# Twelve products without a reader behind layer 0's MLP, and four buffers for the key chunks of the first and the last image

## The chip, the cores and the metric

The kernel runs on one core of one Trainium2 chip. The metric is the time of one execution on the device, in microseconds (us). The time before is the median of three runs; one further execution was taken with the hardware profiler, and all stages below are read from it.

## What is computed

Four images of 192 channels and 64 x 64 pixels go through four layers, one after the other. Cut to what matters here:

```
# layer 0: deformable-convolution queries, channel attention, then an MLP per pixel
xs2 = shortcut + attention(xn)
h1  = layer_norm(xs2, gamma2, beta2)
xs3 = xs2 + gelu(h1 @ w_fc1 + b_fc1) @ w_fc2 + b_fc2        # 192 -> 768 -> 192

# layer 1: non-local attention over all 4096 pixels of an image
g_x, theta_x, phi_x = (conv1x1(x, w, b) for w, b in ...)     # 192 -> 96 each
f   = softmax(theta_x^T phi_x)                                # 4096 x 4096
x   = conv1x1(g_x f^T, W_w, W_b) + x

# layer 2: overlapping-window attention and a gated MLP;  layer 3: a masked depthwise convolution
```

Layer 1 of an image needs all of layer 0's output of that image.

## The kernel before, in words

All arithmetic is float32. The images are taken one after the other, but the layers of neighbouring images are woven together: while layer 1 of image b runs, the gathers of layer 0 for image b+1 run beside it (`weave`); while layers 2 and 3 of image b end (`rest`), the MLP of layer 0 for image b+1 (`mlp0`) is taken a step at a time between their pieces. Image 0's MLP has nothing beside it.

`mlp0` (from L688) goes over eight chunks of 512 pixels. `attend` (L715 to L731) adds the attention's output, a norm follows, `widen` (L796, L803) makes 768 hidden channels with a Gelu on ScalarE (L809), and `narrow` brings them back to 192. `narrow(1)` makes the last 64 channels (L821), `narrow(0)` the first 128 (L818: six products of 128 x 512); each ends with one VectorE instruction (L825) that reads the product's PSUM tile `p` and adds bias and residual into `x`. The PSUM tiles come from a pool of five buffers. After `narrow(0)` the chunk is written to the table `x_flat` in device memory by three DMAs on SyncE's queue (L844).

`keys` (from L849) reads that table back in eight chunks of 512 pixels: each a tile `xk` of 96 x 2 x 512 from the pool `l1k`, loaded by one DMA of 384 KB on SyncE's queue (L855). Of a chunk it makes the keys `ph` (`tp`, L858: two products of 96 x 512, copied out by ScalarE at L859) and the values `gx` (`g`, L863: eight products of 96 columns, copied out by VectorE at L866). Each float32 product shows as two PE instructions in the profile. A buffer of `l1k` is free when the last product of its chunk has read it, and only then can the load that takes its place be issued[...].

In images 1 and 2 the norms of the next image's `offsets` are made between the chunks of `keys` (L360 to L348) from loads of their own (L431). In images 0 and 3 `keys` runs alone. `layer1` follows: its input chunks `xc` (L899), the queries `th` (L902, copied at L904), the scores `s` (L910, copied out by ScalarE at L912), running maxima on VectorE (L915, L917), exponentials and the products with `gx` (L976).

The order of the instructions on each engine is made by a planner, from the order in the program, the data that each needs and its own costs; parts of layer 2's code are kept in the order written. The planner does move work ahead: products of `layer1` (`th`) stand between the chunks of `keys` in the trace. Waits and the reuse of memory are worked out from the tiles.

`ident` is a 128 x 128 identity matrix and `bias` a constant of 128 x 384 (layer 2's position bias, loaded from 174 to 213 us of the span); both stay in SBUF for the whole kernel.

Of the kernel before, what the change touches and what calls it, by code (L numbers as in the profile page):

```python
# [18 lines left out]
B, C, H, W = 4, 192, 64, 64  # L19
# [6 lines left out]
NCH = 8  # L26
# [53 lines left out]
def conv_seq_kernel(ctx: ExitStack, tc: tile.TileContext, a, out: bass.AP):  # L80
    nc = tc.nc

    def pool_of(**kw):

        return tc.tile_pool(**({} if kw.get("space") == DRAM else {"reuse_waits": "tile"}), **kw)
# [7 lines left out]
    def const(shape, name):  # L93
        return wpool.tile(shape, F32, tag=name, name=name)
# [40 lines left out]
    ident = const([128, 128], "ident")  # L135
# [382 lines left out]
    def gather(b, s, at, m2, kept=None):  # L518
# [166 lines left out]
            nc.scalar.copy(m2[rows, C + 2 * M + Q * q : C + 2 * M + Q * q + Q], pm[rows, M:C])  # L685
        yield

    def mlp0(b, m2, pool, sb, ps):  # L688


# [4 lines left out]
        def parts(sb, at, dram, to):  # L695

            yield sb[:, 0 : 2 * at], dram[0:M, to : to + 2 * at]
            for q in range(2):
                yield sb[Q * q : Q * q + Q, 2 * at :], dram[M:C, to + at * q : to + at * q + at]

        def load(i):
            x = xs[i] = pool.tile([M, 3 * HN], F32, tag="x", name=f"xa_{b}_{i}", bufs=2)
            for to, of in parts(x, HN, a["x"][b].rearrange("c h w -> c (h w)"), CN * i):
                nc.sync.dma_start(out=to, in_=of)
# [6 lines left out]
        def attend(i):  # L711

            x, xn = xs[i], xns.pop(i)
            p = ps.tile([128, CN], F32, tag="h", name=f"o_{b}_{i}_0")
            nc.tensor.matmul(  # L715
                p.rearrange("p (r c) -> p r c", c=W), lhsT=m2[:, 0:M], rhs=xn[:, 0:8, 1:65], start=True, stop=False,
                skip_group_check=True,
            )
            for q in range(2):
                nc.tensor.matmul(  # L720
                    p[:, bass.ts(q, HN)].rearrange("p (r c) -> p r c", c=W), lhsT=m2[:, C + M * q : C + M * q + M],
                    rhs=xn[:, 8:12, 1:65], start=False, stop=True, skip_group_check=True,
                )
            nc.vector.tensor_tensor(x[:, 0:CN], x[:, 0:CN], p, ALU.add)
            p = ps.tile([128, CN], F32, tag="h", name=f"o_{b}_{i}_1")[:, 0:HN]
            for q in range(2):
                nc.tensor.matmul(
                    p[Q * q : Q * q + Q].rearrange("p (r c) -> p r c", c=W), lhsT=m2[:, M:C], rhs=xn[:, 4 * q : 4 * q + 4, 1:65],
                    start=True, stop=False, skip_group_check=True,
                )  # L730
            nc.tensor.matmul(  # L731
                p.rearrange("p (r c) -> p r c", c=W), lhsT=m2[:, C + 2 * M :], rhs=xn[:, 8:12, 1:65], start=False, stop=True,
                skip_group_check=True,
            )
            nc.vector.tensor_tensor(x[:, CN:], x[:, CN:], p, ALU.add)
            if i + 1 < NCH:
                load_normalized(i + 1)
            norms[i] = norm_steps(x, i)
# [39 lines left out]
        def norm(i, upto=None):  # L778
            return links(norms[i], upto) if i < NCH else None
# [7 lines left out]
        for i in range(NCH):  # L787
            x = xs.pop(i)
            gl = pool.tile([128, 6, CN], F32, tag="gl", name=f"gl_{b}_{i}")

            def widen(ms):

                banks = [ps.tile([128, 2, HN], F32, tag="h", name=f"h_{b}_{i}_{ms[0]}_{q}") for q in range(2)]
                for j, m in enumerate(ms):
                    for q in range(2):
                        nc.tensor.matmul(  # L796
                            banks[q][:, j, :], lhsT=fc1[:, 0, bass.ts(m, 128)], rhs=hn[:, bass.ts(q, HN)], start=j == 0,
                            stop=False, skip_group_check=True,
                        )
                for j, m in enumerate(ms):  # L800
                    for q in range(2):
                        rows = slice(Q * q, Q * q + Q)
                        nc.tensor.matmul(  # L803
                            banks[q][:, j, :], lhsT=fc1[rows, 1, bass.ts(m, 128)], rhs=hn[rows, CN:], start=False, stop=True,
                            skip_group_check=True,
                        )
                for j, m in enumerate(ms):
                    for q in range(2):
                        nc.scalar.activation(  # L809
                            gl[:, m, bass.ts(q, HN)], banks[q][:, j, :], AF.Gelu, bias=fc1_bias[:, m : m + 1]  # L810
                        )

            def narrow(k):

                p = ps.tile([128, CN], F32, tag="h", name=f"o2_{b}_{i}_{k}")[:, 0 : HN if k else CN]
                for m in range(6):
                    if k == 0:
                        nc.tensor.matmul(p, lhsT=fc2[:, m, 0:M], rhs=gl[:, m, :], start=m == 0, stop=m == 5)  # L818
                        continue
                    for q in range(2):  # L820
                        nc.tensor.matmul(  # L821
                            p[Q * q : Q * q + Q], lhsT=fc2[:, m, M:C], rhs=gl[:, m, bass.ts(q, HN)], start=m == 0, stop=m == 5
                        )
                to = x[:, CN:] if k else x[:, 0:CN]
                nc.vector.scalar_tensor_tensor(to, p, VW["l0_bfc2"][:, k], to, ALU.add, ALU.add)  # L825


            if i + 1 < NCH:
                attend(i + 1)
            widen((0, 1))  # L830
            yield
            norm(i + 1, MEAN)
            widen((2, 3))
            norm(i + 1, SQUARE)
            yield
            widen((4, 5))
            norm(i + 1, VARIANCE)
            narrow(1)
            norm(i + 1, INVERSE)
            yield  # L840
            hn = norm(i + 1)
            narrow(0)
            for of, to in parts(x, HN, x_flat[b % 2], CN * i):
                nc.sync.dma_start(out=to, in_=of)  # L844
            if i + 2 < NCH:
                load(i + 2)
            yield
# [464 lines left out]
    def of_pair(x, j):  # L1312

        return x[:, bass.ts(j, UN)].rearrange("p (h n) -> p h n", h=2), x[:, 4 * UN + CN * j : 4 * UN + CN * j + CN]

    def half(h):
        return slice(Q * h, Q * h + Q)
# [542 lines left out]
    for b in range(B):  # L1860
        with ExitStack() as s:
            sb = s.enter_context(pool_of(name="l1x", bufs=1))
            ph = sb.tile([P, HW], F32, name=f"ph_{b}", tag="ph")
            gx = sb.tile([128, HW // 128, P + 1], F32, name=f"gx_{b}", tag="gx")
            beside, m2, at = None, None, at_second
            if b + 1 < B:
                m2 = stats.tile([M, C + 3 * M], F32, tag="m2", name=f"m2_{b + 1}")
            with ExitStack() as s2:
                making = keys(
                    b, ph, gx, s2.enter_context(pool_of(name="l1k", bufs=2)),  # L1870
                    s2.enter_context(pool_of(name="l1kps", bufs=2, space=PSUM)),
                )
                if 0 < b < B - 1:
                    parts = offsets(b + 1, sb)
                    for _ in range(NCH):
                        next(parts)
                        next(making, None)
                    at = links(parts)
                for _ in making:
                    pass  # L1880
            if b + 1 < B:
                beside = weave(b + 1, at, m2)
            layer1(b, (ph, gx), beside)
        begun.close()
        sums = stats.tile([M, 12], F32, tag="sums", name=f"sums_{b}")
        x = big.tile([M, UNITS * UN + 2 * 2 * 10 * (W + 2)], F32, tag="x", name=f"x_{b}")
        others = x[:, UNITS * UN :].rearrange("p (v k r c) -> p v k r c", v=2, k=2, c=W + 2)

        def load_image():
            for j in range(NCH // 2):  # L1890
                lo, hi = of_pair(x, j)
                for h in range(2):
                    of = x_flat[b % 2][:, bass.ts(2 * j + h, CN)]
                    nc.sync.dma_start(out=lo[:, h], in_=of[0:M])
                    nc.sync.dma_start(out=hi[half(h)], in_=of[M:C])

        oi = big.tile([P, 2, HW], F32, tag="x", name=f"oi_{b}")
        windows(b, oi, load_image)
        held = [oi]
        del oi  # L1900
        rest(b, x, others, held, sums, m2)
        del x, others
# [74 lines left out]
```

## Time and profile before

| | us |
|---|---|
| median of three runs | 7006.99 |
| the three runs | 6996.74, 7006.99, 7022.0 |
| the profiled execution | 6945.72 |
| its span, first to last instruction | 6943.9 |
| PE busy in the span | 6255.0 (90%) |
| VectorE, ScalarE, GpSimd busy | 4819.6, 3728.4, 2070.6 |
| mean granted PE clock | 0.928 |

The four places where an image's MLP ends and its keys begin, from the timeline of PE:

| image | last MLP product ends | L825 that reads it ends | first key product | PE idle between |
|---|---|---|---|---|
| 0 | 801.65 | 802.44 | 807.09 | 5.44 |
| 1 | 2358.64 | 2359.73 | 2367.81 | 9.17 |
| 2 | 3995.75 | 3996.84 | 4004.89 | 9.14 |
| 3 | 5613.61 | 5614.70 | 5621.22 | 7.61 |

How to read the lines in the next part: a timeline line has start and length in us, the engine, the line of code, the operation, output<-inputs, shapes and a count, and in brackets the idle time ahead of it with what ended it. A line of the windows table has the stage, its length, the busy time of PE, PEld (weight loads), DVE, ACT and POOL with instruction counts, the granted PE clock (1.00 is full), the share of the DMA engines' time and GB/s. PE and PEld are TensorE, DVE is VectorE, ACT ScalarE, POOL GpSimd, SP SyncE.

### The profile page before, as it was taken

The page shows a single profiled execution, that of the slowest core. Times are in us where ns is not written, and L with a number is a line of the kernel's source. Part 1 is how long each engine was busy: PE and PEld are TensorE (multiplying, and loading weights), DVE is VectorE, ACT ScalarE, POOL GpSimd, SP SyncE. Part 2 cuts the span into 40 slices and gives each one's busy share as a digit, 9 for nine tenths or more (in the row PEclk, how much of TensorE's full clock was granted, in tenths as well). Part 3 has the DMA queues.
Part 4 walks back from the last instruction along what each step waited for, and adds up shares of the span by engine and source line. Part 5 has one row for each costly group of instructions (what it writes and reads, how often), then busy time and mean ns, then how long its engine had stood idle before and what let it go on. Part 6 is the DMA issues. An engine that isn't in the chain of part 4 may idle for free.

```text
span 6943.9 us, 114885 instructions
## 1 busy us (share of the span) xinstructions
PE 6255.0 (90%) x45020; PEld 4231.5 (61%) x45020; DVE 4819.6 (69%) x7087; ACT 3728.4 (54%) x6214; POOL 2070.6 (30%) x2273
## 2 busy tenths in 40 slices
PE   7878999998987899999988889999998889999876
PEld 4545588885543468886644458887654457766532
DVE  3763199975677669984586849995577757755656
ACT  3763288864444368873544348884544325545331
POOL 2762077732200057751200017772210000012100
PEclk8889899998999899998989999999999979999998
DMA  7993267731010287761010067773010010010000
GB/s 234 302 350 115 74 196 231 232 118 35 24 29 14 72 258 222 231 196 35 10 42 14 28 215 221 226 230 96 13 30 21 19 48 12 12 36 12 4 7 20
DMA packets 362108, 743.43 MB, mean 107 GB/s; under 512 B 52647, under 2 KB 245335, under 8 KB 360798
## 3 DMA queue, kind: packets, MB, share of 16 engines
q0 software_dynamic: 95616, 469.38, 21.0%
q1 hardware_dynamic: 265950, 266.70, 12.9%
q8 instruction: 355, 5.82, 0.3%
q14 instruction: 187, 1.53, 0.1%
HBM read 628.06 MB, written 106.21 MB: 106 GB/s over the span
## 4 chain that ended last, share of the span: by engine, by line
PE 63%; DVE 19%; ACT 7%; DMA 6%; issue 4%; SPq 1%; POOL 0%; DVEq 0%; ACTq 0%; POOLq 0%
PE s L910 11%; PE y L976 10%; PE h L590 6%; DMA ring<-table,idx 3%; PE v L1139 2%; PE qk L1064 2%; DVE ha L1308 2%; PE qk L1065 2%; PE h L1508 2%; DVE ga L1308 2%; PE t L1147 1%; PE tp L858 1%; PE po L482 1%; DVE gate L1308 1%; DVE row L579 1%
## 5 line engine op out<-in xcount | busy, mean ns | idle before, releaser
L572 POOL DMA_INDIRECT ring<-table,idx x1188 | 1673.2, 1408 | 1019.5 <-DVE row L579 235.0
L910 PE MATMUL s<-ths,ph 96*128 96x256 f32 x4096 | 981.8, 385 | 9.0 <-ACT sc L912 4.3
L910 PEld LDWEIGHTS s<-ths,ph 96*128 96x128 f32 x4096 | 782.6, 193 | 148.6 <-ACT ths L904 16.9
L578 ACT ACTIVATE row<-ring,pos 128x384 f32<-128x384 f32 x1188 | 699.0, 610 | 252.6 <-DVE xo L583 159.3
L579 DVE SCALAR_TENSOR_TENSOR row<-ring,fr,row 128x384 f32<-128x384 f32 x1188 | 699.2, 613 | 115.9 <-ACT row L578 109.9
L976 PE MATMUL y<-sc,gx 128*97 128x256 f32 x3008 | 720.1, 379 | 0.0
L976 PEld LDWEIGHTS y<-sc,gx 128*97 128x97 f32 x3008 | 489.0, 164 | 125.7 <-issue 2.3
L582 ACT ACTIVATE xo<-row,pos 128x192 f32<-128x192 f32 x1188 | 503.8, 448 | 74.5 <-DVE row L579 42.4
L583 DVE SCALAR_TENSOR_TENSOR xo<-row,fr,xo 128x192 f32<-128x192 f32 x1188 | 463.9, 410 | 40.3 <-ACT xo L582 38.7
L590 PE MATMUL h<-ti,xo 128*128 128x192 f32 x2376 | 460.6, 329 | 5.8 <-DVE xo L583 5.8
L912 ACT COPY sc<-s 128x1024 f32<-128x1024 f32 x376 | 376.8, 1002 | 158.9 <-PE s L910 157.6
L973 DVE TENSOR_TENSOR sc<-sc,mbs 128x1024 f32<-128x1024 f32 x376 | 446.5, 1216 | 14.0 <-ACT mbs L936 13.7
L917 DVE TENSOR_TENSOR top<-top,sc 128x1024 f32<-128x1024 f32 x282 | 344.5, 1222 | 147.8 <-ACT sc L912 147.3
L590 PEld LDWEIGHTS h<-ti,xo 128*128 128x128 f32 x2376 | 404.7, 191 | 40.1 <-DVE xo L583 12.9
L974 ACT ACTIVATE sc<-sc 128x1024 f32<-128x1024 f32 x376 | 392.9, 1054 | 44.8 <-DVE sc L973 43.0
L1123 DVE TENSOR_REDUCE es<-ex 128x6 f32<-128x384 f32 x264 | 133.3, 546 | 404.2 <-ACT ex L1119 404.2
L1549 POOL COPY gate<-gate 128x192 f32<-128x192 f32 x12 | 4.2, 348 | 1106.1 <-ACT gate L1542 1106.1
L590 PE MATMUL h<-kept,xo 128*128 128x192 f32 x990 | 255.7, 391 | 80.2 <-DVE xo L583 73.4
L1308 DVE SCALAR_TENSOR_TENSOR ga<-gate,v,ga 128x1024 f32<-128x1024 f32 x234 | 299.7, 1281 | 7.2
L590 PEld LDWEIGHTS h<-kept,xo 128*128 128x128 f32 x990 | 180.4, 216 | 167.7 <-DVE xo L583 135.9
L976 PE MATMUL y<-se,gx 128*97 128x256 f32 x1088 | 260.4, 379 | 0.5 <-ACT yn L982 0.5
L1187 POOL TENSOR_TENSOR ot<-ot,ot 102x128 f32<-102x128 f32 x80 | 54.9, 699 | 624.0 <-ACT ot L1181 623.7
(384 smaller groups left out, 11615.0 us busy)
## 6 DMA issues: line engine op xcount, KB each, us to landing
ti<-table SPq DMA_DIRECT2D x396, 96.0 KB
table<-tt SPq DMA_DIRECT2D x24, 1056.0 KB
ring<-table,idx POOLq DMA_INDIRECT x1188, 5.1
xnd<-xn SPq DMA_DIRECT2D x4, 3270.0 KB
table<-kept SPq DMA_DIRECT2D x12, 1056.0 KB
table<-tt SPq DMA_DIRECT2D x44, 288.0 KB
xi<-in_x_dram SPq DMA_DIRECT2D x32, 384.0 KB
xk<-xd SPq DMA_DIRECT2D x32, 384.0 KB
```

Source lines behind the costliest of these rows:

```text
L572: nc.gpsimd.indirect_dma_start(out=gt.rearrange("p r q c -> p (r q c)"), out_offset=None, in_=table[:, :], in_offset=bass.IndirectOffsetOn ...
L578: nc.scalar.activation(row, gt[:, :, 0, :], AF.Copy, scale=pos[:, t, 9 + tap : 10 + tap])
L579: nc.vector.scalar_tensor_tensor(row, gt[:, :, 1, :], fr[:, t, 9 + tap : 10 + tap], row, ALU.mult, ALU.add)
L582: nc.scalar.activation(xo[:, j, :], row[:, 0, :], AF.Copy, scale=pos[:, t, tap : tap + 1])
L583: nc.vector.scalar_tensor_tensor(xo[:, j, :], row[:, 1, :], fr[:, t, tap : tap + 1], xo[:, j, :], ALU.mult, ALU.add)
L590: nc.tensor.matmul(acc[m // 2][:, bass.ts(m % 2, C)], lhsT=xo.rearrange("p j c -> p (j c)")[:, bass.ts(m, 128)], rhs=tt, start=t == 0 and ...
L910: nc.tensor.matmul(p[:, t, :], lhsT=ph[:, bass.ts(G * g + t, 128)], rhs=ths[i], start=True, stop=True)
L912: nc.scalar.copy(to, p)
L973: nc.vector.tensor_tensor(ex, ex, mbs[i].unsqueeze(1).to_broadcast([128, G, QN]), ALU.add)
L974: nc.scalar.activation(ex, ex, AF.Exp)
L976: nc.tensor.matmul(py, lhsT=gx[:, G * g + t, :], rhs=ex[:, t, :], start=g == 0 and t == 0, stop=g == NG - 1 and t == G - 1,)
L1308: nc.vector.scalar_tensor_tensor(acc[:, b], src(tap, b), w[:, tap : tap + 1], acc[:, b], ALU.mult, ALU.add)
```

## The change

Two edits. Behind the last `narrow(0)` of `mlp0`, for every image, twelve products of `ident` with `bias` are written into the PSUM tile of that `narrow`, after L825 has read it. Nothing reads them. And the pool of `keys` gets four buffers in place of two for images 0 and 3; images 1 and 2 keep two.

```diff
+    def keep_warm(p, n):
+
+        columns = bias.rearrange("p e h j -> p (e h j)")
+        for _ in range(n):
+            nc.tensor.matmul(p[:, 0:384], lhsT=ident, rhs=columns, start=True, stop=True)
+
     def mlp0(b, m2, pool, sb, ps):
...
                 to = x[:, CN:] if k else x[:, 0:CN]
                 nc.vector.scalar_tensor_tensor(to, p, VW["l0_bfc2"][:, k], to, ALU.add, ALU.add)
+                return p
...
             hn = norm(i + 1)
-            narrow(0)
+            p = narrow(0)
             for of, to in parts(x, HN, x_flat[b % 2], CN * i):
                 nc.sync.dma_start(out=to, in_=of)
+            if i == NCH - 1:
+                keep_warm(p, 12)
             if i + 2 < NCH:
                 load(i + 2)
             yield
...
                 making = keys(
-                    b, ph, gx, s2.enter_context(pool_of(name="l1k", bufs=2)),
+                    b, ph, gx, s2.enter_context(pool_of(name="l1k", bufs=2 if 0 < b < B - 1 else 4)),
                     s2.enter_context(pool_of(name="l1kps", bufs=2, space=PSUM)),
                 )
```

## The prediction

> **What bounds the kernel now.** I read the page first: PE is busy 90% of the span, and it has 63% of the chain that ended last. But a busy PE is not PE at its peak, so I read next the granted clock (PEclk) by stage, at the four places where layer 0's MLP of an image ends and layer 1's keys of that image begin. The PE timeline at the first of them:
>
> ```profile
> 796.23 5.42 PE L818 MATMUL o<-gl,fc 128*128 128x512 f32 x12
> 807.09 3.73 PE L858 MATMUL tp<-xk,phiT 96*96 96x512 f32 x4 [5.44 <-DMA xk<-xd]
> 810.62 3.57 PE L863 MATMUL g<-gT,xk 96*128 96x96 f32 x16
> ```
>
> PE ends the MLP's last product at 801.65, and waits 5.44 us for the first chunk of the keys. The windows table shows what that gap does to the clock (columns: stage, its length, busy us of PE, PEld, DVE, ACT, POOL, then PEclk, DMA share, GB/s):
>
> ```profile
> 807.00:815.00 8.00, 7.91 (x22) 5.12 (x23) 0.56 (x1) 0.68 (x1) 5.87 (x8) 0.50 1.06 335
> 825.00:835.00 10.00, 10.00 (x37) 7.75 (x36) 0.56 (x1) 1.36 (x2) 0.00 (x0) 0.50 0.15 46
> 855.00:865.00 10.00, 9.26 (x30) 6.67 (x30) 1.11 (x2) 0.68 (x1) 0.00 (x0) 0.50 0.01 2
> 865.00:875.00 10.00, 10.00 (x34) 8.29 (x33) 2.86 (x3) 4.71 (x7) 0.83 (x1) 0.71 0.00 0
> ```
>
> The reader is to see that PE is full and yet stays at half clock for the whole of the keys: their products don't win the clock back; the scores do (0.71). Image 3 is the same, with a gap of 7.61:
>
> ```profile
> 5621.00:5650.00 29.00, 28.78 (x82) 18.86 (x83) 2.23 (x4) 2.73 (x4) 0.00 (x0) 0.50 0.27 74
> 5650.00:5676.00 26.00, 26.00 (x81) 17.96 (x80) 1.91 (x4) 2.73 (x4) 0.00 (x0) 0.50 0.17 52
> ```
>
> Images 1 and 2 have gaps of 9.17 and 9.14, but the norms of the next image's offsets run between the chunks, and the clock returns after some 12 us. From then on it holds through the same products, and through narrower ones:
>
> ```profile
> 2374.00:2380.00 6.00, 6.00 (x12) 2.56 (x12) 0.56 (x1) 0.68 (x1) 0.00 (x0) 0.54 0.23 66
> 2380.00:2390.00 10.00, 9.56 (x66) 6.20 (x65) 3.85 (x6) 3.39 (x4) 0.00 (x0) 1.00 0.43 120
> 2400.00:2410.00 10.00, 10.00 (x68) 6.57 (x67) 5.29 (x7) 4.76 (x8) 0.00 (x0) 1.00 0.43 120
> ```
>
> So in images 0 and 3 the bound is the half clock that the gap left behind. What follows the keys in image 0 is PE again (199 of 200 us busy in 1000 to 1200), so time saved there stays saved.
>
> [...] here a gap of 2.39 us (before L348 at 5569.25) kept the clock. [...]
>
> **Part 1, the 12 products.** Each is a 128x384 f32 product with 128*128 weights and shows as two instructions, as all f32 products here do (L818's 6 show as x12). Price: in the chain, ten of L818's 128x512 take 4.29 us, so 0.429 each, and eight of L976's 128x256 take 1.73, so 0.216: linear in columns. 384 columns: 0.322; 24 of them: 7.7 us at full clock (15.4 at half, the other end). Loads of weights (0.19) hide under them. They write the tile that L825 on DVE reads, so they wait for L825. Behind them on PE are the keys; who waits for those is layer 1. No other PE work is queued there in the trace. They issue no DMA.
> - Image 0: L825 ends at 802.44; PE would run 802.5 to 810.2. The gap left is 0.9 us, so the clock holds. The first chunk is there at 807.09, so it is late by 3.1.
> - Image 1: L825 ends at 2359.73, products end at 2367.5, first chunk at 2367.81: no delay.
> - Image 2: 3996.84, 4004.6, 4004.89: no delay.
> - Image 3: L825 ends at 5614.70, products at 5622.4, first chunk at 5621.22: late by 1.2.
>
> Their cover is the load's flight; without it they would cost 4 x 7.7 = 31 us.
>
> **What the clock is worth.** A chunk of keys at half clock takes 3.41 (4 of L858) + 3.36 (16 of L863) = 6.77 us, eight 54.2. At full clock, from image 1's rows, 1.72 + 1.73 = 3.45, eight 27.6.
> - Image 0: from 807.09 to the first score at 864.05. After: 810.2 + 27.6 + 0.9 (the theta products among them, half of 1.7) + 0.7 (the wait for gx) = 839.4, gain 24.6. The first two score groups at half clock end 3.78 and 3.27 us apart against 1.73 later: 3.2 more. Together 27.8.
> - Image 3: 5622.4 + 27.6 + 1.0 (theta) + 0.6 (its copy) + 0.5 (second load, below) = 5652.1 against 5677.99: 25.9, and 2.6 from the first scores (3.82 and 2.68 against 1.73). Together 28.5.
> - Images 1 and 2: some 12 and 13 us at half clock, so at most 5.8 and 6.5. PE is full from there on, but the second chunks are issued at 2366.95 and 4004.03 and need about 4 us, which is when a faster first chunk ends. I take 5 and 5.5; bounds 0 and the maxima.
>
> Sum: 27.8 + 28.5 + 5 + 5.5 = 67 us.
>
> **Part 2, four buffers.** By itself it is worth nothing at half clock: a buffer's load has 6.8 us and PE never waits after the first chunk. At full clock a chunk takes 3.45 while a load takes 4.2 to 4.3 (802.89 to 807.09; 5616.85 to 5621.22), more beside the 11 gathers that fill DMA from 806 to 825. With two buffers the third chunk would be 1 to 4 us late each time, and the clock in danger; with four, chunks 0 to 3 of image 0 are issued near 803 and needed at 810 to 821, and chunk 4 is issued at 813.7 for 824. I cost the remaining waits at nothing in image 0 (PE has 10 us of work per buffer as cover; uncovered, up to 1 us a chunk) and at 0.5 in image 3, whose second load stays behind an output store on SP until 5621.9. On SP two more loads now stand ahead of layer 1's (L899): those are used 17 us later. [...]
>
> **What is late next.** Image 0: scores and the gather's DVE work, as before. Image 3: scores, then the drain around 5698 (PE idle 3.55 us, clock 0.50) stays.
>
> **The sum and the runs.** The profiled execution took 6945.72 (span 6943.9), 61 below the median shown and below the lowest; I take its stages as valid for the others and subtract: 6945.72 - 67 = 6879 for a profiled run, 7006.99 - 67 = 6940 for the median.
>
> **Rivals.**
> 1. The clock holds over the gap but is lost among the keys (a late load in image 0 beside the gathers, or the 96-column products too thin). For it: the keys can't win the clock back. Against: image 1's 40 us at 1.00 with such products in half of the time. If lost after three chunks: 2 x 3 x 3.3 = 20, plus half of images 1 and 2 (10), less the delay already counted: some 28, so 6979.
> 2. The products don't hold the clock at all; all keys stay at half clock and only the delays of 3.1 + 1.2 remain: 7011. Against: these are full-array rows like L818, which run at 1.00, and L796 at 5593.45 won the clock back within 4 us.
> 3. Slower: the planner puts the 12 products behind the keys' first ones, or the load lands before L825 ends. Then the gap stays uncovered and 7.7 us are paid four times, 7007 + 31 = 7038. It decides at the order of L825 and the load: L825 ended 4.65 us ahead of the first chunk in image 0 and 6.5 to 8.1 in the others, and the products stand first in the program; so a small chance.
>
> **Numbers.** Main case 0.72, rival 1 0.14, rival 2 0.08, rival 3 0.06. The main case's own range is 6922 to 6955: images 1 and 2 from nothing to 12, 2 us on each of the others, and 13 us of scatter, as the three runs show. To hold 8 in 10 the range reaches to rival 1: 6920 to 6980. About 0.3% (21 us) is what a measurement of this kernel can tell from no change. Faster by more: main case and most of rival 1, 0.83; within: rival 2 and the rest of 1, 0.11; slower: 0.06.
>
> **What would show it.** Right: 24 instructions of 0.32 us behind L818 four times; PEclk at 1.00 from the MLP's end to the scores in images 0 and 3; L858's mean at 0.59 for all 128 instead of a median of 1.06; the stage from the first key to the first score 29 instead of 57 us. Wrong: PEclk of 0.50 anywhere in these stages (rivals 1, 2); waits for xk of over 2 us; the new products after a first L858 (rival 3). Also wrong, if the runs without a profile are not at half clock where the profiled one is: then less is to be had.

## The result, and the profile after

| | before | changed |
|---|---|---|
| median, 20 runs each, us | 7007.41 | 6986.08 |
| lowest and highest | 6973.34, 7039.68 | 6937.52, 7005.14 |
| ratio, 95% interval | | 0.996 [0.9941, 0.9978] |
| span of the profiled execution | 6943.9 | 6990.8 |

The change saves 0.4%, some 28 us (15 to 41), where 67 were forecast. The spans of the two profiled executions say nothing on that: the stage up to image 0's last MLP product, whose instructions and order the change doesn't touch, took 801.65 us in one and 849.04 in the other. So the stages are compared, each from the end of the MLP's last product to the first score (in images 1 and 2 to the first `pt` transpose, behind the last chunk of keys). The kernel before was profiled once, in an execution with the short first stage; what its later stages take in one with the long is not known.

| image | before | changed | forecast for the changed kernel |
|---|---|---|---|
| 0 | 62.4 | 60.2 | 38 |
| 1 | 58.7 | 54.8 | 53.7 |
| 2 | 59.3 | 54.5 | 53.8 |
| 3 | 64.4 | 63.4 | 38.5 |

The gain that was forecast for images 0 and 3 isn't there: 2.2 and 1.0 us in place of 24 and 26. In the lines of the changed kernel the keys' products are L867 (`tp`) and L872 (`g`), ScalarE's copy L868, VectorE's copy L875 and the chunk load L864; e2 and e4 have other line numbers, so go by the names there. PE's timeline of the changed kernel in image 0:

```profile
849.88 8.01 PE L692 MATMUL o<-bias,ident 128*128 128x384 f32 x24 [0.84 <-DVE xa L831]
857.73 1.88 PE L867 MATMUL tp<-xk,phiT 96*96 96x512 f32 x4
863.78 2.02 PE L872 MATMUL g<-gT,xk 96*128 96x96 f32 x16 [0.69 <-issue]
869.58 3.52 PE L872 MATMUL g<-gT,xk 96*128 96x96 f32 x16 [2.06 <-DVE gx L875]
872.90 3.62 PE L867 MATMUL tp<-xk,phiT 96*96 96x512 f32 x4
```

The 24 instructions (L692) stand where they should, the first chunk (L867) runs at 1.88 in place of 3.73, and then PE waits 2.06 us in the third chunk. From there on everything takes nearly twice as long again: 3.62 for a chunk's `tp` in place of 1.88, 3.57 for its `g` in place of 1.92. Image 3 goes the same way one chunk earlier:

```profile
5669.95 1.88 PE L867 MATMUL tp<-xk,phiT 96*96 96x512 f32 x4
5671.67 1.92 PE L872 MATMUL g<-gT,xk 96*128 96x96 f32 x16
5675.08 2.99 PE L867 MATMUL tp<-xk,phiT 96*96 96x512 f32 x4 [1.50 <-DMA xk<-xd]
5677.86 3.57 PE L872 MATMUL g<-gT,xk 96*128 96x96 f32 x16
```

The windows table, with the clock in the third column from the right:

```profile
858.00:864.00 6.00, 5.31 (x26) 2.98 (x25) 0.56 (x1) 0.68 (x1) 4.48 (x6) 1.00 1.01 370
870.00:876.00 6.00, 6.00 (x19) 4.09 (x19) 0.56 (x1) 0.00 (x0) 0.00 (x0) 0.50 0.58 175
900.00:906.00 6.00, 6.00 (x18) 3.77 (x18) 0.56 (x1) 0.68 (x1) 0.00 (x0) 0.50 0.44 131
5669.00:5675.00 6.00, 4.59 (x24) 2.96 (x22) 0.56 (x1) 0.68 (x1) 0.00 (x0) 1.00 0.92 229
5675.00:5681.00 6.00, 5.92 (x19) 4.16 (x20) 0.00 (x0) 0.68 (x1) 0.00 (x0) 0.57 0.50 121
5711.00:5717.00 6.00, 6.00 (x21) 4.34 (x20) 0.56 (x1) 0.68 (x1) 0.00 (x0) 0.50 0.00 0
```

So the products carry the clock over the gap, and it is lost inside the keys. Two explanations are open. **Theory W**: a PE wait of 1.5 to 2 us among these thin products takes the clock, and the rest of the keys pays. **Theory T**: the products are too thin to keep it, waits or not.

### The profile page after: what moved, and what is told of

The parts are those of the page before. It is cut to its first block, busy times and chain, and to the rows that moved or that the text cites. A ratio compares the mean times of both kernels' runs of the same rounds, so it can differ in the third digit from the quotient of the medians.

```text
span 6990.8 us, 115078 instructions
## 1 busy us (share of the span) xinstructions
PE 6279.5 (90%) x45116; PEld 4253.4 (61%) x45116; DVE 4816.8 (69%) x7087; ACT 3725.8 (53%) x6214; POOL 2057.9 (29%) x2273
## 4 chain that ended last, share of the span: by engine, by line
PE 62%; DVE 17%; ACT 7%; issue 4%; DMA 4%; SPq 1%; POOL 0%; another core or an unknown queue 0%; DVEq 0%; ACTq 0%; POOLq 0%
PE s L919 12%; PE y L985 10%; PE h L590 6%; PE v L1148 2%; PE qk L1073 2%; PE qk L1074 2%; DVE ha L1317 2%; PE h L1517 2%; DVE ga L1317 2%; PE h L802 1%; PE t L1156 1%; DMA ring<-table,idx 1%; DVE gate L1317 1%; PE zm L1528 1%; PE rb L1222 1%
## 5 line engine op out<-in xcount | busy, mean ns | idle before, releaser
L572 POOL DMA_INDIRECT ring<-table,idx x1188 | 1654.7, 1393 | 1111.2 <-DVE row L579 277.0
L919 PE MATMUL s<-ths,ph 96*128 96x256 f32 x4096 | 997.7, 390 | 15.4 <-ACT ths L913 10.6
L982 DVE TENSOR_TENSOR sc<-sc,mbs 128x1024 f32<-128x1024 f32 x376 | 446.6, 1216 | 20.1 <-ACT mbs L945 13.7
L590 PE MATMUL h<-kept,xo 128*128 128x192 f32 x990 | 266.3, 407 | 111.8 <-issue 54.8
L590 PEld LDWEIGHTS h<-kept,xo 128*128 128x128 f32 x990 | 194.4, 229 | 195.6 <-issue 91.6
L1522 ACT ACTIVATE z<-h,bias_fc1T 128x512 f32<-128x512 f32 x192 | 118.0, 687 | 229.2 <-PE h L1519 228.8
```

Source lines behind the costliest of these rows:

```text
L572: nc.gpsimd.indirect_dma_start(out=gt.rearrange("p r q c -> p (r q c)"), out_offset=None, in_=table[:, :], in_offset=bass.IndirectOffsetOn ...
L590: nc.tensor.matmul(acc[m // 2][:, bass.ts(m % 2, C)], lhsT=xo.rearrange("p j c -> p (j c)")[:, bass.ts(m, 128)], rhs=tt, start=t == 0 and ...
L919: nc.tensor.matmul(p[:, t, :], lhsT=ph[:, bass.ts(G * g + t, 128)], rhs=ths[i], start=True, stop=True)
L982: nc.vector.tensor_tensor(ex, ex, mbs[i].unsqueeze(1).to_broadcast([128, G, QN]), ALU.add)
```

## The experiments

Runs told in one group shared a chip and its runs of the kernel before; ratios are to those. Stages are read as above, images 0 and 3 unless others are named.

### First group: each edit alone, and the waits taken away

**e1, the products alone.**

```diff
-s2.enter_context(pool_of(name="l1k", bufs=2 if 0 < b < B - 1 else 4)),
+s2.enter_context(pool_of(name="l1k", bufs=2)),
```

> The 12 products as in the change, but two buffers for the key chunks in every image. Stage read: from the end of the MLP's last product to the first score, 62.4 us (image 0) and 64.4 (image 3) before, 60.2 and 63.4 in the changed kernel, about 38 if the clock held throughout. Theory W (the products carry the clock into the keys, and PE waits of 1.5 to 2 us among the keys take it again): the third chunk's load can only start when the first chunk is done, so a further wait of 1 to 4 us comes and the clock is gone by the third chunk: 60 to 64 and 63 to 66. Theory T (the keys' thin products lose the clock by themselves after two or three chunks, with or without waits): 58 to 60 in both images. Both: images 1 and 2 as in the changed kernel, about 55, and a total 5 to 20 us below before.

Measured: 0.9962 [0.9941, 0.9984], 26 us (11 to 41); stages 46.1 and 40.7. Both are better than either theory said, and for two reasons that the timeline shows. In image 0 the third chunk did come late, by 5.52 us, and the clock went, but it was back one run of wide products later:

```profile
818.58 3.70 PE L867 MATMUL tp<-xk,phiT 96*96 96x512 f32 x4 [5.52 <-DMA xk<-xd]
822.08 2.03 PE L872 MATMUL g<-gT,xk 96*128 96x96 f32 x16
```

In image 3 the second chunk was late by only 0.56, and the clock stayed at full speed through all eight chunks (1.88 to 1.93 for the `tp` of each):

```profile
5586.01 1.93 PE L867 MATMUL tp<-xk,phiT 96*96 96x512 f32 x4 [0.56 <-DMA xk<-xd]
```

That speaks against T, and asks why four buffers gave 1.50 there (e12). The four stages of this one execution are 45 us shorter than before, more than the runs gained: the clock may not come back in image 0 in every execution.

**e2, the buffers alone.**

```diff
-            if i == NCH - 1:
-                keep_warm(p, 12)
```

> Four buffers in images 0 and 3 and no added products. Both theories: the gap of 5 to 8 us takes the clock before the keys, PE never waits after the first chunk at half clock, so the stages stay at 62 and 64 us and the total is that of before within the scatter (0 +- 10 us).

Measured: 1.0014 [1.0001, 1.0027]; stages 63.1 and 55.2. No gain, as both said. The 55.2 is a surprise: with PE never waiting, the clock came back in the sixth chunk, some 37 us into the keys (3.57 for its `tp`, 1.92 for its `g` behind them). So the keys can win it back, but late and not always.

**e3, the changed kernel without the waits.** Image 3's loads leave by GpSimd's queue; the keys of images 0 and 3 have four PSUM tiles.

```diff
-            nc.sync.dma_start(out=x, in_=x_drams[b % 2][:, :, cols])
+            (nc.gpsimd if b == B - 1 else nc.sync).dma_start(out=x, in_=x_drams[b % 2][:, :, cols])
...
-s2.enter_context(pool_of(name="l1kps", bufs=2, space=PSUM)),
+s2.enter_context(pool_of(name="l1kps", bufs=2 if 0 < b < B - 1 else 4, space=PSUM)),
```

> The changed kernel, with the two waits among the keys taken away: image 3's chunk loads go out on GpSimd's queue, which is idle there, so that the second no longer stands behind an output store that waits for VectorE; and the keys of images 0 and 3 have four PSUM tiles in place of two, so that a late copy no longer holds up PE. Theory W: PEclk 1.00 through the keys of both images, stages of 38 to 41 us, total 50 to 70 us below before. Theory T: no PE wait over 0.5 us among the keys and yet 0.50 from the third chunk on, stages of 58 to 61, total 10 to 25 below before.

Measured: 0.992 [0.9891, 0.9949], 55 us (35 to 75); stages 38.5 and 38.4. The first and the last window of the keys in image 0, then in image 3:

```profile
805.00:811.00 6.00, 6.00 (x32) 3.83 (x31) 0.56 (x1) 1.20 (x2) 4.48 (x6) 1.00 1.02 368
829.00:835.00 6.00, 5.44 (x35) 3.87 (x33) 1.12 (x2) 1.15 (x2) 0.00 (x0) 1.00 0.42 131
```

```profile
5567.00:5573.00 6.00, 6.00 (x32) 3.80 (x31) 0.56 (x1) 1.17 (x2) 1.90 (x3) 1.00 0.59 177
5588.00:5596.00 8.00, 7.96 (x46) 5.35 (x44) 1.67 (x3) 1.37 (x3) 0.00 (x0) 1.00 0.00 1
```

In both images these are the same products, the same number of them, and no wait is above 0.21 us: the clock is at 1.00 to the end. T falls, W stands.

**e4, wide products first, none added.** In images 0 and 3 the `tp` products of four chunks in a row, then the `g` products of these four.

```diff
+        n = 1 if 0 < b < B - 1 else 4
+        for i0 in range(0, NCH, n):
+            ready = [phi(i) for i in range(i0, i0 + n)]
+            for i, x in enumerate(ready):
+                values(i0 + i, x)
+            yield
```

> Without the 12 products, four buffers; in images 0 and 3 the keys' wide products (96 x 512) of four chunks are made in a row and then the thin ones (96 columns) of these four. The gap before the keys stays. If the thin products between the wide ones are why the keys never win the clock back: the first four wide ones, 13.7 us at half clock, bring it to 1.00 within about 7 to 10 us and the rest runs at full clock unless a wait or the run of thin ones loses it: stages of 42 to 48 us, total 30 to 40 below before. If these 96-row products can't win it back in any order: stages of 62 and 64 us, no gain.

Measured: 0.9974 [0.9958, 0.999]; stages 45.5 and 43.5. In image 0 the clock comes back inside the first block of wide products: its 16 instructions take 9.90 us where half clock would take 13.7 and full clock 6.9. That makes about seven at half clock (0.86 us each, 0.43 at full), some 6 us, an estimate from these figures; the 7 to 10 us expected were the author's estimate.

```profile
802.40 9.90 PE L866 MATMUL tp<-xk,phiT 96*96 96x512 f32 x16 [6.34 <-DMA xk<-xd]
812.13 7.28 PE L875 MATMUL g<-gT,xk 96*128 96x96 f32 x64
821.90 10.37 PE L866 MATMUL tp<-xk,phiT 96*96 96x512 f32 x16 [2.48 <-DMA xk<-xd]
```

It is lost again behind the 2.48 us wait of the second block and comes back once more. In image 3 it comes back in the first block too, though a wait of 2.33 us parts the first four instructions (3.73) from the other twelve (7.31, where full clock would take 5.2 and half 10.3); the second block takes 7.03. The stages gained 38 us in the profiled execution, the total only 18 (7 to 29); that difference is not explained.

### Second group: which wait costs which image

**e5, the changed kernel as control.** No edit.

> The changed kernel itself, as a control on the chip of the runs beside it. Theory W (waits of PE among the keys take the clock): image 3 loses it at the second chunk, whose load stands behind the output store, unless the wait comes out shorter than the 1.50 us of before: stage 55 to 63 us, or about 40 if the wait is under 1 us. Image 0: if the copies of VectorE and ScalarE are late again, as in the changed kernel's first profile (1.5 to 3.2 us late at 863 to 869), 60; if that belonged to that execution, about 39. Total 20 to 55 us below before. If the 12 products lost the clock for another reason: no wait over 1 us and yet 0.50.

Measured: 0.9979 [0.9962, 0.9995], 15 us, less than the 20 to 55 expected; stages 59.1 and 63.5, so the loss of the clock is no accident of one execution. Image 3's wait is 1.47 us. Image 2 had a wait of 2.07 in this execution and lost the clock for a while too (3.70 for the `tp` behind it, 1.92 for the `g` after that): 58.5 in place of 54.5. Image 0 on three engines:

```profile
870.50 1.92 PE L872 MATMUL g<-gT,xk 96*128 96x96 f32 x16
872.26 1.88 PE L867 MATMUL tp<-xk,phiT 96*96 96x512 f32 x4
873.69 9.66 SPq L864 DMA_DIRECT2D xk<-xd  x3
873.69 0.56 DVE L875 COPY gx<-g 128x384 f32<-128x384 f32 x1 [12.81 <-PE g L872]
874.31 2.02 PE L872 MATMUL g<-gT,xk 96*128 96x96 f32 x16 [0.17 <-issue]
880.79 2.22 PE L872 MATMUL g<-gT,xk 96*128 96x96 f32 x16 [1.56 <-DVE gx L875]
```

VectorE's copy of the first `g` starts at 873.69, though that product ended about 872.4 by PE's line. VectorE was idle, and SyncE's load (SPq marks its issue), which waits for the same product, is issued in the same instant. So it isn't VectorE that is late: the end of the product reaches both late. (The profile models the ends of PE's instructions, so it doesn't tell whether the product or only its signal was late.) With two PSUM tiles the next `g` then waits for the copy, and 1.56 us in the third chunk took the clock.

**e6, the queue alone** (e3's first edit).

> The changed kernel with one part of e3: image 3's chunk loads on GpSimd's queue, PSUM as in the change. Theory W: image 3 38 to 40 us at 1.00, in every execution; image 0 as in the control beside it. Total at or below the control, 30 to 55 us below before. Rival (the PSUM tiles did it for both images): image 3 as in the control.

Measured: 0.9931 [0.9904, 0.9958]; stages 59.1 and 38.4. As theory W said, image 3 keeps the clock and image 0 is as in the control.

**e7, the PSUM tiles alone** (e3's second edit).

> The changed kernel with the other part of e3: four PSUM tiles for the keys of images 0 and 3, loads as in the change. Theory W: image 0 38 to 40 us, image 3 as in the control (its wait is for a load, which PSUM doesn't change). Total 20 to 45 us below before. Rival (the queue did it for both): image 0 as in the control.

Measured: 0.9955 [0.9934, 0.9976]; stages 39.0 and 62.7. The copies were late in this execution too: the second chunk's `g` products end about 880.8, and their copy starts at 885.11. With four tiles PE's longest wait is 0.36 us:

```profile
878.91 1.92 PE L872 MATMUL g<-gT,xk 96*128 96x96 f32 x16
885.11 1.02 DVE L875 COPY gx<-g 128x384 f32<-128x384 f32 x2 [6.65 <-PE g L872]
885.00 1.95 PE L867 MATMUL tp<-xk,phiT 96*96 96x512 f32 x4 [0.36 <-issue]
```

So it was the tiles that kept the clock, and not an execution without late copies. The two waits are independent, one in each image: the load in image 3 (25 us), the late copies in image 0 (20 us).

**e8, e3 with two buffers.**

```diff
-s2.enter_context(pool_of(name="l1k", bufs=2 if 0 < b < B - 1 else 4)),
+s2.enter_context(pool_of(name="l1k", bufs=2)),
```

> e3 with two buffers for the key chunks in place of four: what the four are worth when nothing else holds PE up. Theory W: image 0's third chunk is issued only when the first is done, beside the gathers, so PE waits some 4 to 6 us for it as in e1 (5.52), loses the clock and wins it back at the earliest within the next chunk: stage 46 or more, up to 62; image 3, with an idle DMA, has a load in about 3.5 us and 3.5 us to hide it: waits under 1 us, 39 to 42. Total 25 to 45 below before, and 8 to 25 above e3. Rival (the four buffers are worth nothing): equal to e3.

Measured: 0.9971 [0.9954, 0.9988], 20 us, a little less than expected; stages 65.0 and 41.5. Image 0 waits for its third chunk and doesn't recover this time; image 3's waits are 0.88 at most and cost only themselves (1.93 for the `tp` behind each):

```profile
879.55 3.70 PE L867 MATMUL tp<-xk,phiT 96*96 96x512 f32 x4 [6.23 <-DMA xk<-xd]
883.04 3.57 PE L872 MATMUL g<-gT,xk 96*128 96x96 f32 x16
```

So the four buffers are needed in image 0, where the loads run beside the gathers, and hardly in image 3.

### Third group: again, a smaller dose, and images 1 and 2

**e9, e3 again.**

> The kernel of e3 once more, as the control of the two runs beside it and to see whether it holds on whichever chip comes. Theory W: both stages 38 to 41 us, images 1 and 2 at 54 to 57, total 0.7 to 0.9% below before. If e3's full hold was the luck of one chip: image 0 or 3 back at 58 or more.

Measured: 0.9923 [0.99, 0.9946], 54 us; stages 39.7, 53.9, 54.1 and 38.4.

**e10, e3 with six products.**

```diff
-                keep_warm(p, 12)
+                keep_warm(p, 6)
```

> e3 with 6 products in place of 12 (3.9 us), so that they end 4.7 us behind the MLP's last product in image 0 and some 5.0 in the others, with gaps of about 1, 2.5 and 4 us left to the first chunk in images 0, 3 and 1 and 2. Theory W (it is the length of the PE gap that decides): image 0 keeps the clock (stage 36 to 40), images 1 and 2 lose it as before (57 to 59), image 3 is the open one: a gap of 2.5 us behind 3.9 us of full rows, 38 if it is kept and up to 62 if lost. Rival (any products behind the MLP keep the clock, whatever gap follows): images 1 and 2 at 54 to 56.

Measured: 0.9947 [0.9928, 0.9965]; stages 53.6, 59.0, 59.1 and 36.8. The gaps left behind the products, image 1 and then image 3:

```profile
2441.95 3.73 PE L867 MATMUL tp<-xk,phiT 96*96 96x512 f32 x4 [3.88 <-DMA xk<-xd]
5695.35 1.96 PE L867 MATMUL tp<-xk,phiT 96*96 96x512 f32 x4 [1.03 <-DMA xk<-xd]
```

3.88 us lose the clock (3.77 in image 2 too), 1.03 keep it, and image 0's 1.40 kept it as well, for four chunks. So it is the gap that decides, and not that products stood there. The miss is image 0: late copies made PE wait 1.90 in the fourth chunk and took the clock there (3.55 for its `g` in place of 1.92), in spite of four PSUM tiles, which had left a wait of 0.36 in e7. Image 3's gap was less than the 2.5 expected: with the load on GpSimd's queue the first key starts 6.3 us behind the MLP's last product (5695.35 after 5689.03), against 7.6 in the kernel before (5621.22 after 5613.61), where the load was issued on SyncE's 3.2 us behind that product (5616.85).

**e11, images 1 and 2 on GpSimd's queue too.**

```diff
-            (nc.gpsimd if b == B - 1 else nc.sync).dma_start(out=x, in_=x_drams[b % 2][:, :, cols])
+            (nc.gpsimd if b else nc.sync).dma_start(out=x, in_=x_drams[b % 2][:, :, cols])
```

> e3 with the chunk loads of images 1 and 2 on GpSimd's queue too (their two buffers unchanged). There the second chunk's load stands behind the output store as well, and PE waits 1.2 to 2.1 us for it, which in the control e5 cost image 2 its clock once (58.5 us in place of 54). Theory W: that wait goes, images 1 and 2 at 51 to 55 us each and never at 58, total 2 to 8 us below e9. If the wait doesn't matter there, since the norms beside the keys bring the clock back: as e9.

Measured: 0.9943 [0.9923, 0.9963]; stages 40.7, 52.4, 52.1 and 38.4. The stages of images 1 and 2 are 2 us shorter than in e9; the total doesn't show it, and lies above e9 within the intervals. In e9 the waits in question were only 0.64 and 1.01 us and kept the clock, so the loss that the edit was to prevent didn't arise. Inconclusive.

### The last run: do the four buffers cost image 3 its clock?

**e12**

```diff
-name="l1k", bufs=2 if 0 < b < B - 1 else 4
+name="l1k", bufs=4 if b == 0 else 2
...
-name="l1kps", bufs=2, space=PSUM
+name="l1kps", bufs=4 if b == 0 else 2, space=PSUM
```

> The 12 products; image 0 with four buffers and four PSUM tiles (as e7), image 3 with two buffers, its loads on SyncE's queue as in the change. The question is whether the four buffers themselves cost image 3 its clock: in the changed kernel, e5 and e7 the second chunk's load has two more right behind it and takes 5.6 to 5.8 us from issue to first use (PE waits 1.29 to 1.50), in e1 with two buffers it took 4.9 (wait 0.56). If the loads behind it slow it: wait 0.4 to 0.9, PEclk 1.00, image 3's stage 40 to 43 us, total 0.5 to 0.9% below before. If e1's short wait belonged to its chip: wait of 1.3 to 1.5 again and a stage of 62 to 64 on a chip whose first key of image 0 comes near 865, and the total as e7 (0.45% below).

Measured: 0.9928 [0.9895, 0.996]; stages 39.3 and 40.9. SyncE's line in image 3 for 4 us from the second load's issue, and PE's lines:

```profile
5657.77 0.68 SPq L864 DMA_DIRECT2D xk<-xd  x1
5662.70 1.93 PE L867 MATMUL tp<-xk,phiT 96*96 96x512 f32 x4 [0.59 <-DMA xk<-xd]
5664.46 1.92 PE L872 MATMUL g<-gT,xk 96*128 96x96 f32 x16
```

and of the changed kernel, SyncE's line for the same 4 us:

```profile
5669.31 2.32 SPq L864 DMA_DIRECT2D xk<-xd  x3
```

From the issue of the second load to its first use: 5657.77 to 5662.70, 4.9 us with two buffers; 5669.31 to 5675.08, 5.8 us with four, where two more loads are issued within 1.8 us behind it. The 0.9 us in between are the difference between a wait of 0.59 that costs about its own length, and one of 1.50 that costs 22. e7, whose image 3 differs from e12's in the buffers alone, had a wait of 1.29 and 62.7 us, on another chip. In image 3 the second edit of the change undid the first.

## Why the prediction was wrong, step by step

**Right.** These parts came out: that PE stood full at half clock through the keys (0.50); that the products cover all four gaps with the clock at 1.00; their price, 7.85 us from 849.88 to the first key against 7.7; their delays; a chunk at full clock (3.47 from 805.09 to 808.56 in e3, against 3.45); images 1 and 2 (3.9 and 4.8 us against 5 and 5.5, the rest being waits of 1.16 and 1.32 us for the second chunk); the order, which is that of before apart from the products, the theta products of image 0 (now behind the keys) and the chunk loads. With the two waits gone the sum holds too: e3's stages are 23.9, 2.5, 5.2 and 26.0 shorter, 57.6 together against 61 forecast for them, and the runs of e3 and e9 give 55 and 54. Two small sums don't come out as written (the first scores give 3.6 and 3.0 us, not 3.2 and 2.6; rival 1 gives 26, not 28); neither matters here.

**Wrong: the remaining waits.** This is the step that failed. The prediction put them "at nothing in image 0" and "at 0.5 in image 3". They were 0.69 and 2.06 in image 0, 1.50 in image 3. The larger error is in what a wait was taken to cost: its own length. Among these products it costs the clock, and so the rest of the keys: 20 us in image 0 (e5 against e7) and 25 in image 3 (e5 against e6). The rival that was given 0.14, the clock lost after some three chunks by a late load beside the gathers or by thin products, named 6979; 6986.08 was measured. It was right that the clock goes among the keys; the late load was image 3's, not image 0's, where late copies did it, and thin products alone were not enough. That its number comes so near is in part luck: the profiled stages give 12 us, not 28.

**Wrong: four buffers as pure gain.** It was seen that the second load stays behind an output store (in the kernel before it is issued at 5621.91, behind the store at 5620.60); it was not seen that with four buffers two more loads follow it at once and lengthen its flight from 4.9 to 5.8 us (e12). In image 0 the buffers do what was said (e8).

**Wrong: the evidence used against the rival.** Image 1's 40 us at 1.00 showed that the clock holds through thin products without waits, and that is so; it said nothing of waits. The gap of 2.39 us that kept the clock stood between products of other shapes, with 128 rows of weights (L821, L348). Of the waits at full clock among the keys' own products, in the PE timelines of the changed kernel, of e4 to e12 and of images 0 and 3 of e1 and e3, every one up to 1.10 us kept it and every one from 1.46 lost it. In between, 1.16, 1.32 and 1.36 kept it, and 1.13, 1.17, 1.21 and twice 1.29 lost it. The least that lost it (e8, image 2) and the greatest that kept it (e11, image 0):

```profile
4079.50 2.97 PE L867 MATMUL tp<-xk,phiT 96*96 96x512 f32 x4 [1.13 <-DMA xk<-xd]
884.74 1.93 PE L867 MATMUL tp<-xk,phiT 96*96 96x512 f32 x4 [1.36 <-DMA xk<-xd]
```

So from 1.13 to 1.36 us the length alone doesn't decide, and what else does was not tested. Four of the five losses there are in images 1 and 2, where the norms stand between the chunks: the clock was back by the next `g` (1.92). In e8's image 2 that cost 2.9 us: 1.13 of wait, 2.97 in place of 1.93 for the `tp`, and 2.58 in place of 1.88 for L360 behind it.

**Open.** Why the ends of products reach the other engines late in image 0 (1.3 us in e5, 4.3 in e7). It goes with the moment in which the DMA engines are full (a share of 0.96 to 1.06 from 857 to 872 in the changed kernel, in windows of 3 us), but e3, whose share is 1.02 from 805 to 811 and 1.04 from 811 to 817, had none of it: its copy starts at 808.76, when the product has ended. The executions that have it also show ScalarE waits whose releaser the profile doesn't know (65.0 us in the changed kernel, none in before or in e1 to e4) and a first stage of 849 to 865 us in place of 796 to 802. Nothing was tried on the cause. Also open is where in the keys the other, unprofiled executions lose the clock: the changed kernel's stages account for 12 us, its runs for 28. In e1, e2 and e4 it is the other way round: the stages are 45, 9 and 38 us shorter, while the runs are 26 and 18 faster in e1 and e4 and 10 slower in e2. These are the executions in which the keys won the clock back by themselves; that they don't in every execution would fit, but is not shown.

**The better version.** e3 (0.992 and 0.9923 in two groups) and e12 (0.9928) are faster than the kernel before; the changed one has 0.996 and 0.9979. They were not run beside the changed kernel, and their intervals overlap that of its 0.996, so their lead over it rests on the stages. e12 needs no second queue.

## What to carry to other kernels

Carrying the clock into a stage is half of the work: among the products of these keys one wait of 1.5 us, and at times one of 1.13, gave it back. So in a stage of such products look for the first load behind a store, the copy that frees a PSUM tile, and anything that is issued right behind the load that is needed next. Price a PE wait in such a stage at the stage's remaining length, not at its own: in e5 waits of 1.56 and 1.47 us cost 20 and 25. And test two edits of one change one at a time: here more buffers helped one image and cost the other the gain of the first edit.

## What the runs showed of the hardware that was not expected

The keys can win the clock back by themselves: in e1 within 3.7 us behind a 5.52 us wait, in e2 only after some 37 us, in image 0 of e8 and e5 not at all. In e4, where wide products stand in a row, it came back in both images, after some 6 us of them in image 0. What decides when it comes back was not shown.
